# A macaron layer on one core: 24 pauses of GpSimd, ahead of the gathers of row 2 and the transfers of rows 2 and 3, are taken out

## The chip, the core and the metric

The kernel runs on one core of a Trainium2 chip. The time is the device time of one execution in microseconds (us). Nine executions of the kernel before lie between 742.82 and 747.31 us, with a median of 744.16 us.

The core has a tensor engine (PE), a vector engine (DVE), a scalar engine (ACT), GpSimd (POOL) and a sync engine (SP). Each takes its own list of instructions in order and waits on semaphores for the others. POOL issues the transfers whose rows are picked by an index (DMA_INDIRECT); SP and, at the ends, ACT issue the plain ones.

## What is computed

The input is 8 rows of 512 tokens of 128 numbers. Three sublayers follow each other, each with a layer norm ahead of it and a residual sum behind it. The first and the last are the same mixture of 8 experts; the middle one is linear attention.

```python
x = x + 0.5 * ffn(layernorm(x))      # 8 experts, the best 2 for each token, 128 -> 512 -> 128
x = x + attn(layernorm(x))           # rms norm; q, k expanded to [1, x, x*x/sqrt2]; 8 heads of 16
x = x + 0.5 * ffn(layernorm(x))      # the same weights again

def ffn(x):                          # probs = softmax(x @ gate_w.T + gate_b)
    h = relu(x @ w1[e] + b1[e])      # for the 2 best experts e of a token
    return sum(prob[e] * (h @ w2[e] + b2[e]))
def attn(x):                         # q, k, v = x @ w_q, x @ w_kv
    return ((q2 @ (k2.T @ v)) / max(q2 . sum(k2), 1e-5)) @ w_out
```

## The kernel before

**Tokens go through HBM, sorted by expert.** For each pair of rows (`Route`, from line 572 on) the kernel works out which two experts each token needs and its place in that expert's region. Then POOL writes the normed tokens into the buffer `xg` in HBM, 128 tokens to an indirect transfer (line 660): a pair of rows has 2 x 4 blocks of tokens x 2 experts, so 16 transfers. `Tiles` reads the regions back 256 tokens at a time (`rows`, line 802, issued by SP), loads the two matrices of the tile's expert (`load`, lines 816 and 818, also SP), transposes (L827), multiplies with both matrices (L843, L858), transposes back (L867) and weighs by the gate (L869). The first sublayer's results are written to the buffer `yt` by SP (L880), the last sublayer's by POOL with indirect transfers (L885).

**The middle.** When a set of rows of the first sublayer is stored, `fetch` (from line 1114 on) gathers each row's two results from `yt` with 8 indirect transfers (line 1125) into a buffer `got`, of which there are two, so the gathers of row b wait until row b-2 has been added. `added` (L1139, DVE) adds them to x; `ready` norms x for the attention; `Attention.prep` makes k, v and q; `squares` (L1018 on PE, L1022 on ACT) makes the squared features of q; `core` sums k with v in 64 small matmuls (L1035) and applies them (L1064, L1066); `quotient` (L1077 on PE, L1080 to L1082 on DVE) and `tail` (L1099 to L1107) divide, project and add to x. Rows 0 and 1 form one set of the first sublayer, rows 2 to 7 another. The last sublayer has one set of 8 rows, planned in three steps: the first step takes rows 0 to 3, the next two rows more, and the last all eight.

**The pause.** `pace()` (line 399) issues a memset of an unused tile of 128 x 192 numbers on POOL (line 402) whenever `clock.paced` is true. It is called ahead of each indirect transfer to `xg` (line 659) and ahead of each gather (line 1124). `PACED = (True, False)`: it is on while the tiles of the first sublayer run and, by line 1227, through the whole attention; it is off for rows 0 and 1 of the first sublayer and while the tiles of the last sublayer run. The memset waits for nothing but POOL itself, so the pause that belongs to a transfer runs as soon as POOL has finished the instruction before it, even where the transfer then waits for a long time.

**The order of the work** is laid down by a planner that runs while the program is built. The work is cut into streams (Python generators); `Clock.look` keeps a time for each engine from fixed costs, and the streams are advanced where their inputs are due (`deal`, `drain`, and a loop over `main` and `side` during the attention). Its costs for POOL are 1.27 us for an indirect transfer out of or into these buffers, and 0.4 us for any other instruction of POOL, the pause among them:

```python
                elif moved:
                    cost = 0.38 if e != "Pool" else 1.9 if outs[0].bass_ap.tensor.name.startswith("x_all") else 1.27
...
                else:
                    cost = 0.4
```

What the planner lays down is then fixed: at the end each instruction is tied to the one before it on its engine. So a change to POOL's list can also change where the instructions of the other engines stand.

Of the kernel before, what the change touches and what calls it, by code (L numbers as in the profile page):

```python
# [36 lines left out]
STAGES = ((4, "rows"), (3, "load"), (2, "turn"), (1, "first"), (0, "second"), (-1, "back"))  # L37
# [10 lines left out]

AHEAD = 2
EARLY = 0.5  # L50
REST = 192

SPARE = (2, 3)
# [7 lines left out]
def macaron_kernel(ctx: ExitStack, tc: tile.TileContext, x, gamma, w_q, w_kv, w_out, gate_wT, gate_b, w1, b1T, w2, b2, out):  # L61
# [49 lines left out]
    class Clock:  # L111
# [1 line left out]


        def __init__(self):
            self.lead, self.paced = LEAD, False
# [199 lines left out]
    def plan_constants():  # L316
        pb1 = psum_misc("pb1")
        nc.tensor.transpose(pb1[0 : E * NC, 0:P], b1s.rearrange("p e c -> p (e c)"), ident)
        nc.vector.memset(b1T32, 0.0)
        nc.vector.tensor_copy(b1T32[0 : E * NC, :], pb1[0 : E * NC, 0:P])  # L320
        nc.vector.tensor_copy(iota_n, iota_i)
        nc.vector.tensor_scalar(iota_2, iota_n[0:1], 2.0, None, ALU.mult)


        nc.vector.tensor_scalar(qi[:, 1:2], qi[:, 0:1], NC.bit_length() - 1, None, ALU.arith_shift_right)
        nc.vector.tensor_scalar(qi[:, 2:3], qi[:, 0:1], NC - 1, None, ALU.bitwise_and)
        nc.vector.tensor_copy(qf, qi)
# [12 lines left out]
        nc.vector.tensor_scalar(which, qf[:, 1:2], float(CAP // N), None, ALU.mult)  # L340
# [55 lines left out]

    rest_area = const.tile([P, REST], F32, name="rest_area")

    def pace():

        if clock.paced:
            nc.gpsimd.memset(rest_area, 0.0)  # L402

    def sent(i, s, g, phase):
# [167 lines left out]
    class Route:  # L572
# [5 lines left out]
        def prep(self):  # L578
# [77 lines left out]
            for t in range(C):  # L656
                for k in range(2):
                    yield "pool"
                    pace()
                    i = nc.gpsimd.indirect_dma_start(  # L660
                        xg[s][g], bass.IndirectOffsetOnAxis(rows[s][:, k, b * T + t : b * T + t + 1], 0), xn[:, t, k], None
                    )
                    sent(i, s, g, phase)

    class Tiles:


        def __init__(self, second, p, prior=None):
            self.s, self.p = int(second), p
            self.g, self.rows_in, self.whole = PHASES[self.s][p]  # L670
            self.prior = prior
            if self.whole:
                self.NF, self.NH = whole_tiles(self.rows_in) - (prior.upto if prior else 0), HALVES
            else:
# [216 lines left out]
    def tiles(ps, pool, steps, routing, sides):  # L891


        spare = SPARE[steps[0].s]
        rest = [(steps[-1], j) for j in range(steps[-1].NF - spare, steps[-1].NF)]
        seq = [(t, j) for t in steps for j in t.order if (t, j) not in rest]
        L = len(seq)
        clock.paced = PACED[steps[0].s]
        kept, keep = [], KEPT[steps[0].s]
        for t in steps:  # L900
            t.ps, t.pool = ps, pool
        for n in range(-4, L + 2):
            if n + 4 < L and (n == -4 or seq[n + 4][0] is not seq[n + 3][0]):
                at = steps.index(seq[n + 4][0])
                drain(routing[at], [s for part in routing[at + 1 :] for s in part])
            if n == -4:

                for t, j in seq[:AHEAD]:
                    t.number(j)
                    t.load(j)  # L910
            open_ones = [s for part in routing for s in part if not s.over]
            for k, (lag, stage) in enumerate(STAGES):
                if 0 <= n + lag < L:
# [6 lines left out]
                if k == len(STAGES) - 1 and (len(kept) > keep or not open_ones):  # L920
                    for u, i in kept[:2]:
                        u.store(i)
                    kept = kept[2:]
                if n >= -1:
                    deal(open_ones + sides)
        while kept:
            u, i = kept.pop(0)
            u.store(i)
        if rest:

            t = steps[-1]
            first = nc.values_load(t.regs[0:1, rest[0][1] : rest[0][1] + 1], min_val=0, max_val=NIL)
            with tc.If(first < NIL):  # L933
                blocks.append(nc.cur_bb.bb)
                for n in range(-4, len(rest) + 2):
                    for lag, stage in STAGES:
                        if 0 <= n + lag < len(rest):
                            getattr(t, stage)(rest[n + lag][1])
                            if stage == "back":
                                t.store(rest[n + lag][1])  # L940
            blocks.append(nc.cur_bb.bb)
            clock.seen = 0

    class Attention:
        def __init__(self, b):
# [168 lines left out]
    def fetch(group):  # L1114

        for u in group:
            b = u.b
            g = set_of[0][b][0]
            yield lambda: all_stored(0, g) and (b < GOT or units[b - GOT].fetched)
            u.got = work.tile([P, 2, T, D], F32, tag="got", name=f"got_{b}", bufs=GOT)  # L1120
            yield "pool"
            for t in range(T):
                for k in range(2):
                    pace()
                    i = nc.gpsimd.indirect_dma_start(  # L1125
                        u.got[:, k, t, :].bitcast(I32), None, yt[0][g].bitcast(I32), bass.IndirectOffsetOnAxis(rows[0][:, k, b * T + t : b * T + t + 1], 0)
                    )
# [167 lines left out]
```

## Time and profile before

| what | us |
|---|---|
| median of nine executions | 744.16 |
| the profiled execution's own time | 745.51 |
| its span, from the first to the last instruction | 743.7 |
| PE busy in the span | 560.7 |
| POOL busy | 306.8 |
| of that: 128 transfers to `xg` (L660) | 132.1 |
| 64 gathers (L1125) | 63.8 |
| 144 pauses (L402) | 39.5 |
| mean granted clock of PE, as a share of full speed | 0.88 |

The stages, in us from the start of the span: the first sublayer's routing and tiles until about 301; the attention from there to 514; the last sublayer's tiles from 518 to about 717; the last sums and the output until the end. Of the 144 pauses, 48 stand ahead of the transfers of rows 2 to 7 to the first sublayer, 64 ahead of the gathers, and 32 ahead of the transfers of rows 0 to 3 to the last sublayer.

How to read the lines of the trace: a row of the timeline has the start, the duration, the engine, the line of the kernel, the operation, what it writes <- what it reads, and the number of instructions merged into it; in brackets stands how long the engine had been idle before it and what ended that. "issue" means that the engine waited for nothing that the profile shows. "PEld" is the loading of weights into PE, and "SPq" is SP's list of instructions.

### The profile page before, as it was taken

The numbers are of one execution on the slowest core, as the hardware profiler recorded it, in microseconds if no ns is written. First come the engines' busy times: TensorE is split into PE (matmuls) and PEld (weight loads), VectorE is DVE, ScalarE is ACT, GpSimd is POOL, SyncE is SP. The second block draws the span as 40 slices with busy tenths as digits, with TensorE's granted clock in tenths as the row PEclk, the third lists the DMA queues.
The fourth block names the chain that finished last, engine by engine and source line by source line (L and its number), as shares of the span: only waits on it lengthen the run. The fifth ranks groups of instructions, "written<-read, shape, count | busy, mean of one in ns | idle before, by whom it ended". The sixth has DMA issues, their size and how long they took to land. (4 is left out here: it accounts for less than half of the span.)

```text
span 743.7 us, 11286 instructions
## 1 busy us (share of the span) xinstructions
PE 560.7 (75%) x3239; PEld 402.8 (54%) x3239; DVE 314.7 (42%) x1186; ACT 265.6 (36%) x587; POOL 306.8 (41%) x452
## 2 busy tenths in 40 slices
PE   3348785389879999878868879977855866999950
PEld 1237664268668888334424425432744744888840
DVE  5616352123264475125934842730532421333325
ACT  3024521024224643316545454525213412444410
POOL 3520828820820000566860390380073374445540
PEclk9999788679979999979998996996786977999995
DMA  4136525347648656111110010012423434787829
GB/s 150 51 107 162 142 85 156 102 128 208 196 125 225 193 157 165 49 36 37 39 38 0 16 40 5 12 44 70 119 84 90 141 121 134 207 226 212 223 63 335
DMA packets 89392, 87.27 MB, mean 117 GB/s; under 512 B 10152, under 2 KB 70832, under 8 KB 89328
## 3 DMA queue, kind: packets, MB, share of 16 engines
q1 hardware_dynamic: 78896, 66.16, 31.4%
q0 software_dynamic: 8320, 17.19, 7.4%
q10 hardware_dynamic: 2112, 3.18, 1.2%
q8 instruction: 27, 0.44, 0.3%
q14 instruction: 37, 0.30, 0.1%
HBM read 62.57 MB, written 23.91 MB: 116 GB/s over the span
## 5 line engine op out<-in xcount | busy, mean ns | idle before, releaser
L660 POOL DMA_INDIRECT xg<-xn_f,rows x128 | 132.1, 1032 | 187.9 <-issue 102.5
L843 PE MATMUL ph_t<-xT_t,w1t_t 128*128 128x256 f32 (+1 forms) x640 | 157.1, 393 | 1.5 <-DMA w1t_t<-in_w_dram 1.0
L858 PE MATMUL py_t<-h_t,w2t_t 128*128 128x256 f32 (+1 forms) x640 | 151.2, 381 | 2.6 <-issue 2.6
L858 PEld LDWEIGHTS py_t<-h_t,w2t_t 128*128 128x128 f32 x640 | 120.8, 201 | 19.4 <-issue 3.4
L843 PEld LDWEIGHTS ph_t<-xT_t,w1t_t 128*128 128x128 f32 x640 | 120.0, 207 | 17.9 <-DMA w1t_t<-in_w_dram 2.9
L1125 POOL DMA_INDIRECT got<-yt,rows x64 | 63.8, 997 | 149.2 <-SPq L933 95.9
L850 DVE TENSOR_SCALAR h_t<-ph_t,bias_t 128x256 f32<-128x256 f32 (+1 forms) x160 | 66.8, 459 | 127.4 <-PE ph_t L843 74.3
L860 ACT ACTIVATE yT_t<-py_t,bias_t 128x256 f32<-128x256 f32 (+1 forms) x80 | 36.6, 457 | 172.1 <-PE py_t L858 114.3
L885 POOL DMA_INDIRECT yt<-y_t,to_t x68 | 65.1, 957 | 76.9 <-DVE to_t L832 54.7
L848 ACT ACTIVATE h_t<-ph_t,bias_t 128x256 f32<-128x256 f32 (+1 forms) x160 | 64.5, 454 | 63.5 <-PE ph_t L843 42.6
L827 PE MATMUL pt_t<-ident,xt_t 128*128 128x128 f32 x148 | 32.6, 300 | 43.7 <-DVE gone_t L778 16.5
L869 DVE TENSOR_TENSOR y_t<-py_t,xt_t 128x256 f32<-128x256 f32 (+1 forms) x80 | 32.2, 403 | 64.5 <-PE py_t L867 49.8
L1035 PE MATMUL pz_a<-fac,v 128*32 128x160 f32 x512 | 36.8, 310 | 18.0 <-issue 16.8
L827 PEld LDWEIGHTS pt_t<-ident,xt_t 128*128 128x128 f32 x148 | 19.0, 150 | 49.1 <-DVE gone_t L778 16.7
L829 ACT COPY xT_t<-pt_t 128x256 f32<-128x256 f32 (+1 forms) x80 | 28.2, 353 | 43.8 <-PE pt_t L827 32.0
L558 ACT ACTIVATE xn_f<-x_all,off_f,rs_w_f 128x256 f32<-128x256 f32 x64 | 32.4, 591 | 30.8 <-DVE off_f L547 30.8
L402 POOL MEMSET rest_area<- 128x192 f32 x144 | 39.5, 274 | 0.1
L1035 PEld LDWEIGHTS pz_a<-fac,v 128*32 128x32 f32 x512 | 18.6, 109 | 36.4 <-issue 33.4
L567 PE MATMUL pt_f<-ident,xn_f 128*128 128x128 f32 x64 | 17.2, 383 | 23.5 <-ACT xn_f L558 18.0
L867 PE MATMUL py_t<-ident,yT_t 128*128 128x128 f32 x148 | 31.0, 286 | 5.0 <-ACT xT_t L829 2.5
L988 DVE TENSOR_TENSOR fac<-fac 128x896 f32<-128x896 f32 x32 | 33.1, 1082 | 0.0
L1080 DVE TENSOR_SCALAR d_a<-pd_a 128x16 f32<-128x16 f32 x16 | 2.7, 171 | 64.3 <-PE pd_a L1077 59.8
(403 smaller groups left out, 706.4 us busy)
## 6 DMA issues: line engine op xcount, KB each, us to landing
w1t_t<-in_w_dram SPq DMA_DIRECT2D x80, 256.0 KB
w2t_t<-in_w_dram SPq DMA_DIRECT2D x80, 256.0 KB
xt_t<-xg SPq DMA_DIRECT2D x68, 130.0 KB
yt<-y_t SPq DMA_DIRECT2D x36, 128.0 KB
xg<-nil SPq DMA_DIRECT2D x27, 130.0 KB
x_all<-in_x_dram SPq DMA_DIRECT2D x8, 256.0 KB
xg<-xn_f,rows POOLq DMA_INDIRECT x128
fac<-yt SPq DMA_DIRECT2D x4, 512.0 KB
```

Of the source, the lines that this page charges most:

```text
L402: nc.gpsimd.memset(rest_area, 0.0)
L660: i = nc.gpsimd.indirect_dma_start(xg[s][g], bass.IndirectOffsetOnAxis(rows[s][:, k, b * T + t : b * T + t + 1], 0), xn[:, t, k], None)
L827: nc.tensor.transpose(pt[:, bass.ts(u, P)], self.x[j][:, u, 0:D], ident)
L843: nc.tensor.matmul(ph[c // 2][:, c % 2, 0:n], lhsT=self.w[j][0][:, bass.ts(c, P)], rhs=self.xT[j], start=True, stop=True)
L848: nc.scalar.activation(h, ph[c // 2][:, c % 2, 0:n], AF.Relu, bias=bias)
L850: nc.vector.tensor_scalar(h, ph[c // 2][:, c % 2, 0:n], bias, 0.0, ALU.add, ALU.max)
L858: nc.tensor.matmul(py, lhsT=self.w[j][1][:, c, :], rhs=self.h[j][c], start=(c == 0), stop=(c == NC - 1))
L860: nc.scalar.activation(self.yT[j], py, AF.Identity, bias=self.bias[:, NC, j : j + 1])
L885: i = nc.gpsimd.indirect_dma_start(yt[self.s][self.g], bass.IndirectOffsetOnAxis(self.to[j][:, u : u + 1], 0), self.y[j][:, u, :], None)
L988: nc.vector.tensor_tensor(out, one, two, ALU.mult)
L1035: nc.tensor.matmul(sums[slot, bass.ts(k, FS)], lhsT=self.v[:, t, 2 * j + k, :], rhs=self.fac[:, t, 2 * j + k, LIN : LIN + FS], start=(t == 0),
L1125: i = nc.gpsimd.indirect_dma_start(u.got[:, k, t, :].bitcast(I32), None, yt[0][g].bitcast(I32), bass.IndirectOffsetOnAxis(rows[0][:, k, b ...
```

## The change

The pause is left out in two places: ahead of the 8 gathers of row 2 (but not of row 3), and ahead of the 16 transfers to the last sublayer of the stream that holds rows 2 and 3. That is 24 of 144 pauses. `pace` gets the row as an argument; for the first sublayer's transfers and the other gathers it is called with -1, which pauses as before.

```diff
+HURRY = 1
...
-    def pace():
-
-        if clock.paced:
+    def pace(b=-1):
+
+        if clock.paced and not (HURRY and b in (2, 3)):
             nc.gpsimd.memset(rest_area, 0.0)
...
                 for k in range(2):
                     yield "pool"
-                    pace()
+                    pace(b if s else -1)
                     i = nc.gpsimd.indirect_dma_start(
                         xg[s][g], bass.IndirectOffsetOnAxis(rows[s][:, k, b * T + t : b * T + t + 1], 0), xn[:, t, k], None
                     )
...
             for t in range(T):
                 for k in range(2):
-                    pace()
+                    pace(b if b == 2 else -1)
                     i = nc.gpsimd.indirect_dma_start(
                         u.got[:, k, t, :].bitcast(I32), None, yt[0][g].bitcast(I32), bass.IndirectOffsetOnAxis(rows[0][:, k, b * T + t : b * T + t + 1], 0)
                     )
```

The rest of the diff adds switches that are set to nothing: `LASTS = (0, 0)` is subtracted in the order of the half tiles, `MID = 0` leaves the list of tiles put aside in the first step empty, the block for the spare tiles becomes a function of its own, and a step's plan also waits (in the planner) for a flag `clock.made`, which is set once the constants have been made.

```diff
-            self.order = sorted(range(self.NT), key=lambda j: j if j < self.NF else (j - self.NF + EARLY) * self.NF / self.NH - 0.5)
+            self.order = sorted(range(self.NT), key=lambda j: j if j < self.NF else (j - self.NF + EARLY) * (self.NF - LASTS[int(second)]) / self.NH - 0.5)
...
-            yield lambda: counted[s][g] == self.rows_in and (not self.prior or self.prior.planned)
+            yield lambda: clock.made and counted[s][g] == self.rows_in and (not self.prior or self.prior.planned)
...
+        early = [(steps[0], j) for j in range(steps[0].NF - MID, steps[0].NF)] if s == 0 else []
+        seq = [(steps[0], j) for j in steps[0].order if (steps[0], j) not in early + rest]
+        cut = len(seq) if early else None
...
         plan_constants()
+        clock.made = True
```

More of the change, by code (lines that the diff above doesn't have):

```diff
@@ L50 @@
 EARLY = 0.5
+LASTS = (0, 0)
+HURRY = 1
+MID = 0
 REST = 192
@@ L115, in __init__ @@
         def __init__(self):
-            self.lead, self.paced = LEAD, False
+            self.lead, self.paced, self.made = LEAD, False, False
             self.seen, self.last, self.link = len(nc.cur_bb.bb.instructions), 0.0, {}
@@ L891, in tiles @@
     def tiles(ps, pool, steps, routing, sides):
-        spare = SPARE[steps[0].s]
-        rest = [(steps[-1], j) for j in range(steps[-1].NF - spare, steps[-1].NF)]
-        seq = [(t, j) for t in steps for j in t.order if (t, j) not in rest]
+        s = steps[0].s
+        rest = [(steps[-1], j) for j in range(steps[-1].NF - SPARE[s], steps[-1].NF)]
+        early = [(steps[0], j) for j in range(steps[0].NF - MID, steps[0].NF)] if s == 0 else []
+        seq = [(steps[0], j) for j in steps[0].order if (steps[0], j) not in early + rest]
+        cut = len(seq) if early else None
+        if early:
+            seq += [None] * 3
+        seq += [(t, j) for t in steps[1:] for j in t.order if (t, j) not in rest]
         L = len(seq)
-        clock.paced = PACED[steps[0].s]
-        kept, keep = [], KEPT[steps[0].s]
+        clock.paced = PACED[s]
+        kept, keep = [], KEPT[s]
         for t in steps:
             t.ps, t.pool = ps, pool
+        begun = None
         for n in range(-4, L + 2):
-            if n + 4 < L and (n == -4 or seq[n + 4][0] is not seq[n + 3][0]):
-                at = steps.index(seq[n + 4][0])
+            if n + 4 < L and seq[n + 4] and seq[n + 4][0] is not begun:
+                begun = seq[n + 4][0]
+                at = steps.index(begun)
                 drain(routing[at], [s for part in routing[at + 1 :] for s in part])
@@ L912, in tiles @@
             for k, (lag, stage) in enumerate(STAGES):
-                if 0 <= n + lag < L:
+                if 0 <= n + lag < L and seq[n + lag]:
                     t, j = seq[n + lag]
@@ L919, in tiles @@
                         kept.append((t, j))
-                if k == len(STAGES) - 1 and (len(kept) > keep or not open_ones):
+                if k == len(STAGES) - 1 and (len(kept) > keep or not open_ones or n == cut):
                     for u, i in kept[:2]:
@@ L925, in tiles @@
                     deal(open_ones + sides)
+            if n == cut:
+                assert not kept
+                spares(early)
         while kept:
@@ L929, in tiles, with spares @@
         if rest:
[L931 to L940, printed above, removed]
-            blocks.append(nc.cur_bb.bb)
-            clock.seen = 0
+            spares(rest)
+    def spares(rest):
+        t = rest[0][0]
+        first = nc.values_load(t.regs[0:1, rest[0][1] : rest[0][1] + 1], min_val=0, max_val=NIL)
+        with tc.If(first < NIL):
+            blocks.append(nc.cur_bb.bb)
+            for n in range(-4, len(rest) + 2):
+                for lag, stage in STAGES:
+                    if 0 <= n + lag < len(rest):
+                        getattr(t, stage)(rest[n + lag][1])
+                        if stage == "back":
+                            t.store(rest[n + lag][1])
+        blocks.append(nc.cur_bb.bb)
+        clock.seen = 0
     class Attention:
```

## The prediction

> **What bounds the kernel now.** I began with POOL's timeline, because the change touches POOL alone. It shows what a pause takes: first in the transfers of rows 2 and 3 to the last sublayer, then in the transfers of rows 4 and 5, which have none.
>
> ```profile
> 489.65 0.27 POOL L402 MEMSET rest_area<- 128x192 f32 x1
> 490.08 0.96 POOL L660 DMA_INDIRECT xg<-xn_f,rows  x1 [0.16 <-issue]
> 491.05 0.27 POOL L402 MEMSET rest_area<- 128x192 f32 x1
> 491.49 0.96 POOL L660 DMA_INDIRECT xg<-xn_f,rows  x1 [0.17 <-issue]
> ...
> 541.11 0.95 POOL L660 DMA_INDIRECT xg<-xn_f,rows  x1 [0.30 <-issue]
> 542.37 0.96 POOL L660 DMA_INDIRECT xg<-xn_f,rows  x1 [0.30 <-issue]
> ```
>
> From start to start it is 1.405 us with the pause and 1.262 without. The memset takes 0.27 us, but POOL is idle for 0.16 to 0.17 us before a transfer instead of 0.30, so a pause costs 0.143 us and not 0.27.
>
> The second view was PE's timeline beside POOL's. One step of the attention, the 64 small matmuls of L1035, shows what POOL's lists do to other engines:
>
> ```profile
> 301.63 2.39 PE L1035 MATMUL pz_a<-fac,v 128*32 128x160 f32 x64 [1.07 <-DVEq L933]
> ...
> 316.39 1.55 PE L1035 MATMUL pz_a<-fac,v 128*32 128x160 f32 x34
> 318.53 0.49 PE L1035 MATMUL pz_a<-fac,v 128*32 128x160 f32 x5 [0.58 <-issue]
> 319.99 0.50 PE L1035 MATMUL pz_a<-fac,v 128*32 128x160 f32 x5 [0.97 <-issue]
> ```
>
> With POOL silent (unit 0, at 301.6) all 64 take 2.39 us. Beside the paced gathers of rows 2 and 3, which run from 305.61 to 327.3, the same step takes from 316.39 to 327.9: PE gets 4 or 5 matmuls, then stands for up to 0.97 us, waiting for nothing that the profile shows. It recurs at 490.96 to 501 beside the transfers of rows 2 and 3. So POOL's lists hold PE back even with pauses, and until they end.
>
> The third view was the windows beside those transfers (columns: PE, PEld, DVE, ACT and POOL busy in us, each with its count; clock; DMA share; GB/s):
>
> ```profile
> 486.00:494.00 8.00, 7.36 (x80) 2.66 (x80) 2.94 (x20) 2.28 (x3) 7.17 (x12) 1.00 0.14 44
> 494.00:503.00 9.00, 5.74 (x31) 2.33 (x28) 2.16 (x13) 0.00 (x0) 7.28 (x12) 0.82 0.16 51
> ```
>
> PE starts 80 matmuls in the first 8 us, 31 in the next 9. Those 31 are little work: 64 of L1035 take 2.39 us, so about 1.2 us.
>
> The fourth view was the chain of waits where the pauses are already missing:
>
> ```profile
> 549.10 0.88 DVE h_t L850 x2
> 549.98 15.30 another core or an unknown queue
> ```
>
> The transfers of rows 4 and 5, without pauses, run from 539.85 to 562.3, and from 549.98 to 564.5 neither PE nor ACT starts anything. That speaks loudest against the change.
>
> Last, SP's waits tell what starts the last sublayer:
>
> ```profile
> SPq L816 <- PE pav_a L1066: 25.9, 1, 25.9
> ```
>
> The weights of its third tile wait until PE has ended the attention's last matmuls, at 514.49. Its first rows are asked for behind that, at 518.19, though the last transfer of rows 2 and 3 was issued by 502.3. So not the transfers but PE's attention sets the start of the last stage; from there to the end PE is the bound (81.0 of 81 us busy from 625 to 706).
>
> **The change, part by part.** The 8 gathers of row 2: POOL ran the first of their pauses at 209.40, ahead of 95.93 us of idle time, so it costs nothing. Seven lie between gathers. The period there is 1.385 us (305.61, 307.00, 308.38); no gather without a pause is in the trace, so I take the gather's 0.95 and the transfers' 0.30 gap, 1.25 us. That is 7 x 0.134 = 0.9 us. Bounds: 0 (row 3's paced gathers follow, and PE's hindrance at 316 to 328 might simply keep its length) and 7 x 0.27 = 1.9 us (the whole memset). I take 0.9: the nearest row, the transfers, gives half of the memset. It lies on the path: row 3's gathers end 0.9 us sooner, and with them the hindrance that holds PE in unit 1's L1035 until 327.9. DVE's sum for row 2 (330.34) stands behind the quotient of unit 0, which waits 15.7 us for PE behind that same step. What is late next is that sum, and behind it the gathers of row 4, which start at 332.02.
>
> The 16 transfers: the first pause ran at 446.34, 29 us before its transfer. Fifteen lie between: 15 x 0.143 = 2.1 us. They end at 500.2 instead of 502.3. Nobody waits for their data (covered by 12 us until 514.49; without that cover it would be the same 2.1 us). But PE is freed from its crawl 2.1 us sooner, with units 6 and 7 still to be finished and the end of them on the path. Bounds: a gain of 15 x 0.27 = 4.1 us, and a loss of 8.1 us, worked out below as the slow rival. I take the gain of 2.1, because the stretch from 494 on is already nearly a standstill, and ending it sooner is what is left to change.
>
> One of these 16 transfers (480.11) takes 5.02 us beside DVE's four multiplications of L988, 4.1 us in all. [...] By the rows alone each list of 16 met one such group of L988, with one transfer held, and the sum stays as it is.
>
> The rest of the diff does nothing: with `LASTS` and `MID` at zero the orders are the same lists, and DVE's constants (L333, at 26.5 us) stand ahead of the first plan's first instruction (L699, at 29.0) already.
>
> The sum: 0.9 + 2.1 = 3.0 us. The profiled execution took 745.51 us, 1.8 around its span of 743.7; it becomes 742.5, with a span of 740.7. It lay 1.35 above the median of nine, so against the median: 744.16 - 3.0 = 741.1 us. With the bounds of a gain (1.9 + 4.1) it is 738.2.
>
> **The rivals.** *The planner lays the work down differently, for the better.* It charges 0.4 us for a pause, so it now sees row 2's gathers 8 x 0.4 = 3.2 us sooner, and may put row 2's sum ahead of the quotient of unit 0. Then it need not wait for PE until 329.5, and POOL loses its pause ahead of row 4:
>
> ```profile
> 332.02 0.95 POOL L1125 DMA_INDIRECT got<-yt,rows  x1 [4.41 <-DVE x_all L1139]
> ```
>
> For it: the sum's data landed about 12 us before it ran. Against it: other engines' lists are full there. Price: 3.0 + 4.4 = 7.4 us, 736.8.
>
> *The order turns out worse.* The same shift moves the steps of L1035 against POOL's lists. Only unit 0's runs free (2.39 us); unit 2's, from 364.14 to 367.1, and unit 6's, from 477.4 to 481.3, get by lightly. One of these falling into a list, as unit 7's does (490.96 to 500.7, 9.7 us), costs about 9.7 - 2.4 = 7.3 us: 744.16 - 3.0 + 7.3 = 748.5. Against it: five of eight already lie there, so there is more to win than to lose.
>
> *Nothing moves.* PE's attention is bound by its own and DVE's work, POOL's earlier end is absorbed, and the first rows of the last stage are asked for at 518 as before: 744.2. For it: the 12 us of cover. Against it: PE stands idle exactly while POOL issues.
>
> *Slower: the full standstill moves into the attention.* Among the transfers without pauses the stop begins 549.98 - 539.85 = 10.1 us after the first and lasts until 2.3 us after the last (562.26 to 564.53). Put on rows 2 and 3 it would reach from 486.0 to 502.5. The work PE did there before, 7.36 us up to 494 and 1.2 after, would follow at 502.5, so what was reached at 503 is reached at 511.1: 8.1 us later. With the 0.9 of the gathers it is 744.16 + 8.1 - 0.9 = 751.4. It decides from the point at which the stop begins: before 494 it costs, from there on the crawl covers it. For it: both lists without pauses beside tiles show such a stop. Against it: those stood beside SP's loads (75 to 127 GB/s, against 28 here), and the held transfer at 480 to 485 gives the others 5 us to catch up; counted from its end, the stop would begin at 485.6 + 10.1 = 495.7, under the crawl.
>
> **How the numbers follow.** The forecast (741.1) 0.33; a better order (736.8) 0.20; nothing (744.2) 0.14; the standstill (751.4) 0.20; a worse order (748.5) 0.13. The likeliest case by itself reaches from 738.2, where each pause is worth its whole memset, to 742.7, where half of the gain is absorbed. The gains hold 0.53 and the losses 0.33; since the losses go further, the range must reach past 748.5 to the standstill's 751.4, and below to the better order's 736.8, a little past each since both are sums: 735.5 to 751.5. A measurement of this kernel can tell about 0.2%, 1.5 us, from no change. Faster by more than that (under 742.7): 0.53. Within it: 0.14. Slower: 0.33.
>
> **What would show it.** Right: 120 memsets of L402; gathers of row 2 at 1.25 us from start to start, transfers of rows 2 and 3 at 1.26; unit 1's L1035 ending near 327 and unit 7's crawl ending about 2 us sooner; SP's wait at L816 ending near 511.5; everything behind it shifted by the same amount. Wrong: a stop of PE of 10 us or more between 476 and 503 (the standstill); a different order of DVE's list around L1139 and L1080 (the planner); or L816 still let go at 514.5 (nothing moves). [...]

## The result, and the profile after

The kernel after takes 753.6 us (median of 20 executions, 747.76 to 757.0) beside 744.16 us for the kernel before (62 executions). The ratio is 1.0134, with a 95% interval of 1.0114 to 1.0153: **9.4 us slower**, and above the range of the prediction. The profiled execution took 750.93 us, with a span of 749.0 us; it has 120 pauses. The lines of the code have moved: L1035 is now L1052, L1064 and L1066 are L1081 and L1083, L660 is L664, L1125 is L1142, L988 is L1005, L816 is L820; in some of the experiments the lines lie 1 to 3 further on. Unit n is the attention of row n.

POOL did what the diff says. Its timeline in the kernel after: row 2's gathers, the first of row 3, and the first transfers of rows 2 and 3.

```profile
304.30 0.95 POOL L1142 DMA_INDIRECT got<-yt,rows  x1 [95.58 <-SPq L950]
305.56 0.94 POOL L1142 DMA_INDIRECT got<-yt,rows  x1 [0.30 <-issue]
...
313.98 0.28 POOL L406 MEMSET rest_area<- 128x192 f32 x1
314.42 0.95 POOL L1142 DMA_INDIRECT got<-yt,rows  x1 [0.17 <-issue]
...
478.43 0.96 POOL L664 DMA_INDIRECT xg<-xn_f,rows  x1 [42.07 <-issue]
479.70 0.95 POOL L664 DMA_INDIRECT xg<-xn_f,rows  x1 [0.31 <-issue]
```

From start to start a gather without a pause takes 1.25 us and a transfer 1.26, as predicted. But the other engines fared differently. Here is PE's timeline for the step of unit 1 beside the gathers (64 matmuls; in the kernel before it lasted from 316.39 to 327.9):

```profile
318.55 1.01 PE L1052 MATMUL pz_a<-fac,v 128*32 128x160 f32 x21
320.61 0.33 PE L1052 MATMUL pz_a<-fac,v 128*32 128x160 f32 x2 [1.05 <-issue]
322.00 0.30 PE L1052 MATMUL pz_a<-fac,v 128*32 128x160 f32 x1 [1.06 <-issue]
...
338.12 1.83 PE L1052 MATMUL pz_a<-fac,v 128*32 128x160 f32 x20 [0.27 <-issue]
```

PE now gets one or two matmuls every 0.7 to 1.4 us, where it got 4 or 5, until POOL's list ends. That list is longer: rows 2, 3 and 4 follow each other without a gap, 24 gathers from 304.30 to 336.1. The windows beside the transfers of rows 2 and 3 (columns as in the prediction's windows of the kernel before):

```profile
486.00:494.00 8.00, 0.11 (x2) 0.00 (x0) 0.00 (x0) 0.00 (x0) 6.17 (x7) 0.50 0.17 58
494.00:503.00 9.00, 1.66 (x7) 1.33 (x8) 0.41 (x3) 0.87 (x2) 3.40 (x4) 0.50 0.09 30
```

PE was busy for 7.36 and 5.74 us of these 8 and 9 us before, and for 0.11 and 1.66 now. The chain of waits says the same of this list, and of the next one, where the kernel before had a stop of 15.30 us too:

```profile
480.14 20.96 another core or an unknown queue
...
555.85 3.09 issue
559.91 15.67 issue
```

A full standstill has come, up to 501.1. SP's wait shows how late the attention ends:

```profile
SPq L820 <- PE pav_a L1083: 13.7, 1, 13.7
```

Its end, PE's last matmuls of L1083, is at 516.3, 1.8 us later than before, while the whole span is 5.3 us longer. So a part of the loss arises behind the attention, where the diff takes out no pause.

The runs below stood on five chips. On two of them the kernel before takes 607 us, and no stop beside a list of POOL's is seen (beside the 16 transfers of rows 2 and 3 PE's longest idle time is 0.85 us in e1); on the others it takes 744 to 759 us ("a chip with stops": PE stands for 15.23 us in the first result and for 14.99 in e13). Each run is compared only with the kernel before on its own chip. In the tables the times are medians of all executions, but the ratios leave out those in a slow state, over 1.5% above the quickest of the same kernel, so that a ratio can differ from the quotient of the times by up to 0.4%.

### The profile page after: what moved, and what is told of

It is laid out like the page before. It is cut to its first block, busy times and chain, and to the rows that moved or that the text cites. A ratio compares the mean times of both kernels' runs of the same rounds, so it can differ in the third digit from the quotient of the medians.

```text
span 749.0 us, 11262 instructions
## 1 busy us (share of the span) xinstructions
PE 546.6 (73%) x3239; PEld 399.4 (53%) x3239; DVE 314.0 (42%) x1186; ACT 264.6 (35%) x587; POOL 295.0 (39%) x428
## 4 chain that ended last, share of the span: by engine, by line
PE 36%; issue 6%; ACT 5%; another core or an unknown queue 5%; DMA 3%; DVE 2%; POOL 1%; SPq 1%; DVEq 0%; ACTq 0%; POOLq 0%
PE ph_t L847 8%; PE py_t L862 6%; PE pz_a L1052 4%; PE pav_a L1081 3%; PE pf_a_rest L1035 2%; PE pav_a L1083 2%; DMA fac<-yt 2%; PE po_a L1122 1%; DMA yt<-y_t,to_t 1%; PE pkv_a L982 1%; PE pt_t L831 1%; PE pd_a L1094 1%; PE pl_f L597 1%; PE py_t L871 1%
## 5 line engine op out<-in xcount | busy, mean ns | idle before, releaser
L664 POOL DMA_INDIRECT xg<-xn_f,rows x128 | 126.4, 988 | 149.3 <-issue 83.0
L847 PE MATMUL ph_t<-xT_t,w1t_t 128*128 128x256 f32 (+1 forms) x640 | 158.1, 394 | 2.9 <-DMA w1t_t<-in_w_dram 2.6
L862 PE MATMUL py_t<-h_t,w2t_t 128*128 128x256 f32 (+1 forms) x640 | 149.5, 378 | 1.7 <-issue 1.7
L847 PEld LDWEIGHTS ph_t<-xT_t,w1t_t 128*128 128x128 f32 x640 | 120.8, 209 | 19.4 <-DMA w1t_t<-in_w_dram 4.2
L862 PEld LDWEIGHTS py_t<-h_t,w2t_t 128*128 128x128 f32 x640 | 119.3, 199 | 17.8 <-issue 2.5
L1142 POOL DMA_INDIRECT got<-yt,rows x64 | 64.2, 1003 | 158.3 <-SPq L950 95.6
L833 ACT COPY xT_t<-pt_t 128x256 f32<-128x256 f32 (+1 forms) x80 | 28.2, 354 | 52.2 <-PE pt_t L831 21.3
L1052 PE MATMUL pz_a<-fac,v 128*32 128x160 f32 x512 | 35.5, 348 | 15.3 <-issue 14.1
L1052 PEld LDWEIGHTS pz_a<-fac,v 128*32 128x32 f32 x512 | 21.2, 124 | 30.3 <-issue 28.6
L406 POOL MEMSET rest_area<- 128x192 f32 x120 | 32.9, 275 | 0.1
L1005 DVE TENSOR_TENSOR fac<-fac 128x896 f32<-128x896 f32 x32 | 32.9, 1084 | 0.0
L871 PEld LDWEIGHTS py_t<-ident,yT_t 128*128 128x128 f32 x148 | 20.5, 147 | 14.4 <-ACT xT_t L833 7.0
```

The costliest lines, as they stand in the source:

```text
L664: i = nc.gpsimd.indirect_dma_start(xg[s][g], bass.IndirectOffsetOnAxis(rows[s][:, k, b * T + t : b * T + t + 1], 0), xn[:, t, k], None)
L847: nc.tensor.matmul(ph[c // 2][:, c % 2, 0:n], lhsT=self.w[j][0][:, bass.ts(c, P)], rhs=self.xT[j], start=True, stop=True)
L862: nc.tensor.matmul(py, lhsT=self.w[j][1][:, c, :], rhs=self.h[j][c], start=(c == 0), stop=(c == NC - 1))
L871: nc.tensor.transpose(pb[:, bass.ts(u, P)], self.yT[j][:, bass.ts(u, P)], ident)
L1052: nc.tensor.matmul(sums[slot, bass.ts(k, FS)], lhsT=self.v[:, t, 2 * j + k, :], rhs=self.fac[:, t, 2 * j + k, LIN : LIN + FS], start=(t == 0),
L1142: i = nc.gpsimd.indirect_dma_start(u.got[:, k, t, :].bitcast(I32), None, yt[0][g].bitcast(I32), bass.IndirectOffsetOnAxis(rows[0][:, k, b ...
```

## The experiments

**What the diff does to the order.** With `HURRY` at 0 the program is that of the kernel before, instruction for instruction, so the rest of the diff is inert. With only the transfers' pauses gone, the order of every other instruction is the one of before as well. With only row 2's gathers' pauses gone it is already that of the kernel after, so the 8 gathers alone make the new order. There are thus two orders and two lots of pauses, and they can be crossed. "Stop" and "order" are the two theories at first.

### Crossing pauses and order

e1: the transfers' pauses alone. e2: the gathers' pauses alone. e3: the new order with all pauses. e4: the gathers' pauses alone, in the old order.

```diff
 e1
-                    pace(b if b == 2 else -1)
+                    pace(-1)
 e2
-        if clock.paced and not (HURRY and b in (2, 3)):
+        if b == 5 or clock.paced and not (HURRY and b in (2, 3)):
...
-                    pace(b if s else -1)
+                    pace(5 if s and b in (2, 3) else -1)
 e3
-                if e not in self.free:
+                if e not in self.free or i.name in self.unseen:
...
+        if clock.paced or b in (2, 3):
+            i = nc.gpsimd.memset(rest_area, 0.0)
+            if HURRY and b in (2, 3):
+                clock.unseen.add(i.ins.name)
 e4
+        elif clock.paced:
+            clock.look()
+            clock.free["Pool"] += 0.4
...
-                    pace(b if s else -1)
+                    pace(-1)
```

> Only the 16 pauses ahead of the transfers of rows 2 and 3 go; row 2's gathers keep theirs, and the order of all instructions is that of the kernel before. Two theories. 'Stop': 16 transfers without pauses bring PE, DVE and ACT to a full stop that lasts until 2 to 3 us after the last of them, and that is the whole loss. It expects a stop from about 484 to 503 in PE, and 750 to 753 us (my price for it of 8.1 us, on 744.2). 'Order': the loss comes from the new order that the planner lays down, and the transfers' pauses matter little. It expects no stop of more than 3 us there and 742 to 744.5 us.

> Only the 8 pauses of row 2's gathers go; the 16 transfers keep theirs. The planner lays all other instructions down as in the kernel after. 'Stop' expects no full stop beside the transfers. At 478 us the kernel after had ended 228 of the attention's 256 matmuls pav_a, the kernel before 196, so with the stop gone this is the quickest so far: 744.2 less some 4 to 10 us, 734 to 740. 'Order' expects the time of the kernel after, 752 to 755.

> All 144 pauses stand, but the planner doesn't count the 24, so every other instruction stands where it stands in the kernel after. This is the new order alone. 'Stop' expects 735 to 741 us, some 1 us above the run with row 2's pauses gone. 'Order' expects 752 to 755.

> The order of the kernel before (the planner still counts 0.4 us where a pause would stand), with the 8 pauses of row 2's gathers left out. Both theories expect little. My prediction's first term: 0.9 us less, 743.3; a third idea, that the 16 gathers from 304 on come to a full stop as well when half of them have no pauses, would cost PE the matmuls L1035 of unit 1 that it ran from 316 to 326, some 2 to 5 us: 746 to 749.

| run, beside before at 607.03 us | us | ratio, 95% interval |
|---|---|---|
| e1 transfers' pauses gone (old order) | 608.59 | 1.0017, 0.9995 to 1.0040 |
| e2 gathers' pauses gone (new order) | 618.72 | 1.0201, 1.0170 to 1.0233 |
| e3 new order, all pauses | 618.26 | 1.0177, 1.0147 to 1.0206 |
| e4 gathers' pauses gone, old order | 606.96 | 0.9993, 0.9964 to 1.0022 |

These stood on a chip of the 607 us kind. In e1 nothing stops: the window over its 16 transfers has PE at work nearly throughout.

```profile
389.00:414.00 25.00, 23.64 (x286) 11.16 (x285) 14.18 (x52) 15.10 (x29) 19.65 (x16) 1.00 0.13 42
```

So "stop" couldn't be tried there; "order" is borne out in its sign (its times were stated for the other kind of chip): the new order alone, with every pause in place, costs 11 us. Where it loses is shown by the same window of e2 and then of e4, in the last stage:

```profile
470.00:500.00 30.00, 22.82 (x109) 17.97 (x107) 11.49 (x58) 7.52 (x18) 22.68 (x25) 0.83 0.66 194
```

```profile
470.00:500.00 30.00, 27.91 (x145) 23.03 (x144) 13.88 (x65) 9.99 (x24) 22.35 (x24) 1.00 0.75 219
```

and by SP's wait for the indirect transfers ahead of the tiles' rows, of e2 and then of e4 (total, times, longest):

```profile
SPq L806 <- DMA xg<-xn_f,rows: 27.5, 9, 16.2
```

```profile
SPq L809 <- DMA xg<-xn_f,rows: 15.5, 11, 3.7
```

The first transfer of rows 4 and 5 starts at 451.99 in e2 and at 437.82 in e4, though the attention ends at the same time (its last matmuls start at 410.7 and 411.4). The gate of these rows (L597, `pl_f`) stands behind the first tile's first matrix (L847) on PE's list in the new order; in the old one it stands ahead of that matrix, right behind the tile's first two transposes. In the kernels before and after it is the same. PE's timeline of before, then of after:

```profile
521.64 0.66 PE L827 MATMUL pt_t<-ident,xt_t 128*128 128x128 f32 x2 [5.28 <-DMA xt_t<-xg]
522.10 3.42 PE L593 MATMUL pl_f<-gwT,xnT_f 128*128 128x8 f32 x16
...
528.69 2.76 PE L843 MATMUL ph_t<-xT_t,w1t_t 128*128 128x256 f32 x8
```

```profile
523.17 1.08 PE L831 MATMUL pt_t<-ident,xt_t 128*128 128x128 f32 x4 [6.33 <-DMA xt_t<-xg]
...
527.07 3.14 PE L847 MATMUL ph_t<-xT_t,w1t_t 128*128 128x256 f32 x8
...
533.58 1.95 PE L597 MATMUL pl_f<-gwT,xnT_f 128*128 128x8 f32 x16
```

Their first transfers of rows 4 and 5 start at 539.85 (before) and 552.49 (after).

### The kernel after again, and the old order without pauses

e5 is the kernel after. e6 has its 24 pauses gone in the old order, e7 all 144; both charge the 0.4 us as e4 does. e8 has all pauses, and the planner counts 0.143 us for each.

```diff
 e7
-        if clock.paced and not (HURRY and b in (2, 3)):
+        if clock.paced and False:
 e8
-                    cost = 0.4
+                    cost = 0.143 if i.name in self.rests else 0.4
```

> The kernel after, unchanged, beside the kernel before. The first four runs stood on a chip on which the kernel before takes 607 us instead of 744, and there the two kernels with the new order lost 1.8 to 2.0% while the transfers' pauses alone cost 0.2%. 'Order' expects, on a chip like that, 1.018 to 1.024 (618 to 621 us), and on one like that of the first result 1.013 again. 'Stop' expects that the part that the stop adds is missing on the 607 us chip: under 1.005.

> All 24 pauses go as in the kernel after, but the planner still counts 0.4 us for each, so all other instructions stand as in the kernel before. 'Order' expects the time of the kernel before on either chip: 0.997 to 1.004. 'Stop' expects the stop's 8 us where the chip shows stops (1.010 to 1.013 of 744 us), and 1.000 to 1.004 where it doesn't.

> The order of the kernel before, and none of the 144 pauses is made. If pauses protect the other engines on this chip, the 120 further ones must cost much: 16 transfers cost 1.6 us, so 48 more ahead of the first sublayer's transfers and 56 ahead of gathers at that price make 10 us or more. If pauses do nothing here but take POOL 0.143 us each, then the time falls or stays: the lists of 32 transfers and 40 gathers end 4.6 and 5.7 us sooner, of which little is waited for: 0.990 to 1.000.

> All 144 pauses stand, and the planner counts 0.143 us for each, which is what one was seen to cost, instead of 0.4. That makes a third order. 'Order' says that the time moves by some per cent for the order alone and that its sign can't be told from POOL's own time: outside 0.995 to 1.005, in either direction. If instead the order that the kernel after has is slow for a reason of its own (row 2's sum early), a mere change of the charge should stay within 0.995 to 1.005.

| run, beside before at 758.63 us | us | ratio, 95% interval |
|---|---|---|
| e5 kernel after | 768.74 | 1.0142, 1.0087 to 1.0198 |
| e6 all 24 gone, old order | 753.06 | 0.9941, 0.9906 to 0.9977 |
| e7 all 144 gone, old order | 774.56 | 1.0198, 1.0129 to 1.0268 |
| e8 a third order, all pauses | 757.16 | 1.0002, 0.9960 to 1.0045 |

This chip shows stops. e6 is the kernel that my sum was made for, and it is quicker: the old order carries the change, the new one doesn't. e5 and e6 lack the same 24 pauses and differ in the order alone, and 768.74 - 753.06 = 15.7 us lie between them. "Stop" had expected a loss for e6 and is off; "order" had expected 0.997 to 1.004, which the interval just reaches. And e8 falls against "any new order moves the time": a third order is worth nothing either way. Its profile has both signs, though: the gate of rows 4 and 5 stands behind the first tile there too (544.16 and 534.84) and all that follows the attention is long, while the attention itself is short (206.6 and 238.8 us, measured as in the last table below). e7 shows that pauses do protect on this chip: without any, the time is 774.56 us beside 758.63, and there are stops beside the gathers too, as in e7's chain of waits:

```profile
358.27 6.47 another core or an unknown queue
```

Why no standstill in e6? Windows over the transfers, of e6 and then of the kernel after:

```profile
486.00:511.00 25.00, 20.03 (x185) 8.49 (x184) 9.70 (x28) 7.93 (x15) 19.70 (x16) 0.91 0.13 41
```

```profile
478.00:501.00 23.00, 5.74 (x76) 2.48 (x72) 0.91 (x6) 0.58 (x1) 15.31 (x16) 0.66 0.14 47
```

The same 16 transfers at the same pace, and PE does 20.03 us of work beside the one and 5.74 beside the other. Two things differ. In e6 the fourth transfer is held beside DVE's four multiplications of `fac`, as it was before; in the kernel after the last of these ran at 466.55 to 470.6, ahead of the list, and no transfer takes over 0.96 us. And the instruction behind PE's step `pe_t`: first POOL's and PE's timeline of e6, then PE's of the kernel after.

```profile
490.51 5.30 POOL L667 DMA_INDIRECT xg<-xn_f,rows  x1 [0.30 <-issue]
```

```profile
497.49 0.19 PE L764 MATMUL pe_t<-take_t,ev_t 33*1 33x9 f32 x2
497.61 0.62 PE L1084 MATMUL pav_a<-sq_a_(0, 0)_5018,zT_a 128*32 128x512 f32 x2
```

```profile
485.91 0.20 PE L761 MATMUL pe_t<-take_t,ev_t 33*1 33x9 f32 x2
501.34 1.12 PE L1116 MATMUL po_t_a<-ident,on_a 128*128 128x128 f32 x4 [15.23 <-DVE regf_t L764]
```

In e6 PE has matmuls of the attention next, which wait for nothing. In the kernel after the next one is let go, by the profile, by DVE's `regf_t`, and DVE starts nothing before 501.13. DVE stands in e6 too (11.41 us, up to 510.36), but PE's next matmuls don't need it. Which of the two differences decides wasn't tried by itself.

### Rows 4 and 5 early, or late

If the place of that gate is what costs, moving it alone should win the time back. e9 keeps the planning loop of the attention going until the gate of rows 4 and 5 is laid down, which brings the attention's last tails ahead of the first tile as well; the transfers' pauses stay gone. e11 does the opposite to the kernel before. e10 repeats e2 and e12 repeats e1.

```diff
 e9
+            if s and b == 4:
+                clock.made = 2
...
-        while not core.over:
+        while not core.over or clock.made != 2:
 e11
-HURRY = 1
+HURRY = 0
...
-            yield lambda: all(u.done for u in units[b : b + n])
+            yield lambda: all(u.done for u in units[b : b + n + (b == 4)])
```

> The kernel after, with one change: the attention's planning loop goes on until the gate's matmuls for rows 4 and 5 of the last sublayer have been laid down, so these stand ahead of the first tile on PE's list, not behind it. 'Late routing' (the new order loses because the transfers of rows 4 and 5 to the last sublayer come 12 to 17 us later, and its second step starves): they should come back by 8 us or more, and the time should fall by 5 to 11 us below that of the kernel after, to a ratio of 0.997 to 1.007. 'Spread' (the new order is worse in many small places): 1.012 to 1.020 stays. 'Stop' (on a chip that shows stops): the stop at 480 to 501 stays and so does the loss, 1.010 to 1.014.

> The new order with row 2's pauses gone and the 16 transfers' pauses kept, as in the second run. On a chip that shows no stops: 1.020 again. On one that does, where the kernel after is at 1.013 to 1.014: 'Stop' expects that the standstill ahead of the last sublayer goes with the pauses back, and the ratio falls below 1.005. 'Late routing' expects that the ratio stays at 1.010 or more, since the transfers of rows 4 and 5 come as late as before.

> The kernel before with all 144 pauses, and the planner lets the routing of rows 4 and 5 to the last sublayer begin only when unit 6 is finished too, not with units 4 and 5. That puts its gate's matmuls behind the first tiles, later still than in the kernel after. Attention up to its last matmuls is laid down as before. 'Late routing' expects 1.015 to 1.035, more than in the kernel after as the transfers come later still. 'Spread' and 'Stop' expect little, under 1.008.

> The order of the kernel before, the 16 transfers without pauses, as in the first run. On a chip without stops 1.000 to 1.004 again. On one with stops, where both lots of pauses gone in this order gave 0.994: my prediction's second term expects 2.1 of those 4.5 us from here, 0.996 to 0.998; if it's the gathers that gave all of it, 0.999 to 1.003; 'Stop' expects 1.008 or more.

| run, beside before at 756.90 us | us | ratio, 95% interval |
|---|---|---|
| e9 after, gate of rows 4 and 5 early | 758.51 | 1.0037, 1.0002 to 1.0072 |
| e10 new order, transfers paced | 766.24 | 1.0167, 1.0114 to 1.0221 |
| e11 old order, gate late | 757.92 | 1.0053, 1.0009 to 1.0097 |
| e12 old order, transfers not paced | 758.75 | 1.0053, 1.0009 to 1.0098 |

The kernel after itself was not run on this chip. Beside its 1.2 to 1.4% on the others, e9 has won most of the loss back. e10 shows that the new order stays slow with the transfers' pauses back, as "late routing" had it and "stop" not. But e11 misses: its transfers of rows 4 and 5 start 27 us later than in e12 (the first at 575.99 and 548.79), and it loses 0.5%, not 1.5 to 3.5%. So lateness alone isn't the price. Nor is PE's wait for the first rows alone: in e11 it is 6.41 us, with the last tails and the gate behind it as in the kernel after, and yet e11 takes 232.4 us from the attention's last matmuls to the end, beside 237.8 in e10 and 231.5 in e12.

e12 falls between the stated ranges: not the gain that my second term had, and a smaller loss than "stop" expected. Its loss of 0.1 to 1.0% is barely clear of nothing (over all executions the medians differ by 0.2%). No standstill is in it: over the same window as e6, PE is busy for nearly as long.

```profile
486.00:511.00 25.00, 19.76 (x184) 8.19 (x182) 10.24 (x30) 7.59 (x15) 19.66 (x16) 0.88 0.13 41
```

### Both edits on one chip

e13 is the kernel after, e14 has the transfers' pauses back, e15 the gate early, and e16 both.

> The kernel after, beside the next three on one chip. 1.013 to 1.014 where the chip shows stops (measured twice); where it doesn't, 1.018 to 1.022, as the two other kernels with this order had there.

> The kernel after with the 16 transfers' pauses back. 'Stop' expects it 0.5 to 1% quicker than the kernel after on a chip with stops. 'Late routing' expects no gain against it, within 0.4% either way, since the paced transfers hold PE back nearly as much and the last stage starts its routing as late.

> The kernel after with the gate of rows 4 and 5 laid down ahead of the first tile. 'Late routing' expects it 7 to 11 us quicker than the kernel after on the same chip, of either kind: 1.002 to 1.006 with stops, 1.003 to 1.010 without. If that gain came only from the chip on which it was measured, it lies within 4 us of the kernel after.

> Both edits: the gate of rows 4 and 5 early, and the 16 transfers' pauses back (only row 2's gathers without). 'Stop' expects 5 to 8 us less than the run without these pauses on a chip with stops, which would be 0.993 to 0.997 and the quickest kernel. 'Late routing' expects the same time as that run, within 3 us.

| run, beside before at 743.59 us | us | ratio, 95% interval |
|---|---|---|
| e13 kernel after | 753.11 | 1.0117, 1.0068 to 1.0165 |
| e14 and transfers paced | 748.09 | 1.0089, 1.0049 to 1.0129 |
| e15 and gate early | 745.13 | 1.0028, 0.9993 to 1.0063 |
| e16 and both | 741.40 | 0.9961, 0.9924 to 0.9997 |

The early gate is worth 753.11 - 745.13 = 8.0 us, or 748.09 - 741.40 = 6.7 with pauses; the intervals overlap in neither pair, and "late routing" had expected 7 to 11. The transfers' pauses are worth 5.0 or 3.7 us; here the intervals overlap in both pairs, but taken directly from the executions of the two kernels the means differ by 4.5 and 3.9 us, each with a standard error of 1.3. That is what "stop" expected of e14; of e16 it expected 5 to 8 us, and "late routing" at most 3, so both miss there. Together 11.7 us, and **e16 is quicker than the kernel after**, and than the kernel before by 0.4% (0.03 to 0.76%, barely clear of nothing). What the early gate does is seen in PE's timeline of e13 and then of e15:

```profile
520.76 0.66 PE L1116 MATMUL po_t_a<-ident,on_a 128*128 128x128 f32 x4
527.74 1.09 PE L831 MATMUL pt_t<-ident,xt_t 128*128 128x128 f32 x4 [6.32 <-DMA xt_t<-xg]
...
537.72 1.95 PE L597 MATMUL pl_f<-gwT,xnT_f 128*128 128x8 f32 x16
```

```profile
517.58 0.66 PE L1118 MATMUL po_t_a<-ident,on_a 128*128 128x128 f32 x4
...
523.98 1.95 PE L597 MATMUL pl_f<-gwT,xnT_f 128*128 128x8 f32 x16
...
527.85 0.63 PE L833 MATMUL pt_t<-ident,xt_t 128*128 128x128 f32 x2
```

In e13 PE stands 6.32 us for the first rows of the last stage, with the last tails of the attention and the gate behind them. In e15 this work fills the wait, and the first transfer of rows 4 and 5 goes out at 541.02, not 556.66. What the pauses do is in the windows of e13 and then e14 over the 16 transfers:

```profile
484.00:506.00 22.00, 5.17 (x72) 2.36 (x68) 0.91 (x6) 0.58 (x1) 15.03 (x16) 0.69 0.15 49
```

```profile
482.00:506.00 24.00, 13.11 (x126) 7.47 (x122) 3.28 (x18) 2.02 (x4) 19.10 (x31) 0.67 0.13 44
```

### The two terms in the old order

e17 repeats e4, and e18 repeats e6.

> The order of the kernel before, only the 8 pauses of row 2's gathers gone. My prediction's first term: 0.9 us less, 0.998 to 1.000. If the gathers made the whole gain of the kernel that has none of the 24 pauses, on a chip with stops: 0.990 to 0.996. On one without stops 0.999 again.

> The order of the kernel before, all 24 pauses gone. My prediction's sum: 3.0 us less, 0.996, as the first such run gave (0.994). If the transfers' pauses cost 0.5% when they go, as the other run has it, this lies 0.3 to 0.6% above the run beside it; if 'Stop' and the gathers cancel, 0.998 to 1.002. On a chip without stops 0.998 to 1.003.

They came to a chip of the 607 us kind (before 607.35): e17 606.52 us, 0.9992 (0.9969 to 1.0014), and e18 607.54 us, 1.0011 (0.9988 to 1.0034). There the 24 pauses are worth nothing that can be measured. The gathers alone, in the old order, were not run on a chip with stops.

### The stages in the profiles

Each profile gives two lengths: from row 2's first gather to the start of the attention's last matmuls (L1066 and its later lines), called the attention here, and from there to the end, called the last stage. Means, in us, on the chips with stops (without e7, e8 and e11, whose pauses or orders are others):

| stage | kernels | mean (lowest to highest) |
|---|---|---|
| attention | old order: before, e6, e12 | 209.2 (207.8 to 210.9) |
| attention | new order, transfers not paced: after, e5, e9, e13, e15 | 215.6 (210.9 to 219.4) |
| attention | new order, transfers paced: e10, e14, e16 | 209.9 (208.4 to 212.4) |
| last stage | old order: before, e6, e12 | 231.4 (230.3 to 232.4) |
| last stage | new order: after, e5, e10, e13, e14 | 234.9 (231.9 to 238.0) |
| last stage | new order, gate early: e9, e15, e16 | 227.6 (227.1 to 228.1) |

From the old order to that of the kernel after, the attention gets longer by 215.6 - 209.2 = 6.4 us, of which 215.6 - 209.9 = 5.7 go when the transfers have their pauses back; these I put down to the standstill. The last stage gets longer by 234.9 - 231.4 = 3.5. Together 9.9 us, beside the 9.4 of the result. These are single profiles from several chips, and the ranges are some us wide, so it is partly luck that the sum comes out this close. On one chip alone, the attention takes 214.5 and 214.2 us in e13 and e15, and 208.4 and 209.0 in e14 and e16, with the pauses back. On the 607 us chip of the first four runs the attention is equally long in e1, e2 and e4 (161.7 each; 163.6 in e3), and the last stage takes 204.3 and 204.6 us in e2 and e3 against 195.1 and 196.1 in e1 and e4: the loss lies there.

## Why the prediction was wrong, point by point

- **The pause's cost** (0.143 us a transfer, 0.134 a gather) was right, to 0.01 us.
- **The step that failed first is the frame of the sum: it was made in the order of before.** I knew that the planner would see row 2's gathers 3.2 us sooner, but I left a new order to the rivals. The new order comes from the planner's charge alone (e3). In the order that the sum was made for, the change gained 0.6% or 4.5 us on a chip with stops (e6; 0.2 to 0.9%), where I forecast 3.0, and nothing on a 607 us chip (e18). The same 24 pauses gone, the new order takes 15.7 us more (e5 against e6).
- **Term A (0.9 us):** row 2's gathers did end sooner. But PE's hindrance in unit 1 didn't end with them; it lasts to 339.88 now and not to 327.9, since row 4's gathers follow without a gap. Where the term was tried in the old order, on the 607 us chips, it is within noise (e4, e17).
- **Term B (2.1 us)** failed: "the stretch from 494 on is already nearly a standstill, ending it sooner is what is left to change". In the new order PE's standstill began 7.7 us after the first transfer (478.43 to 486.1), and the pauses' return was worth 3.7 to 5.0 us. In the old order the kernel without these pauses alone lost 0.5% (0.1 to 1.0) on one chip (e12), where this term forecast a gain; e6, without the gathers' pauses as well, gained on another. The 31 matmuls from which I priced the loss are not all of L1035; 26 are.
- **The standstill rival** named the event and its window (486.0 to 502.5 forecast; 486.1 to 501.3 measured for PE). That the start fits so well is luck: the list began 2.5 us later than before, and the stop 2.4 us sooner after it. Its size was put too high (8.1 us against 5.7, 5.0 or 3.7). I set against it that the held transfer gives the others 5 us to catch up. In the old order, with the held transfer, there was indeed no standstill (e6, e12); in the new order no transfer was held, and it came. That the held transfer is the reason isn't shown.
- **The held transfer.** In each list of 16 I counted on one transfer held beside DVE's four multiplications, as in the kernel before (5.02 us); in e6 it took 5.30. In the kernel after none of the 16 was held, each took 0.96 us at most: the multiplications had ended at 470.6, 7.8 us ahead of the list. With one transfer held PE did 20.03 us of work in 25 (e6), with none 5.74 in 23. What holds such a transfer, no run here shows.
- **A better order** came in its mechanism and not in its gain. DVE's sum for row 2 did move ahead, to 316.48, and POOL's 4.41 us of idle time are gone. But PE only got a longer list of gathers to crawl beside, and the quotient of unit 0 (L1080, now L1097) came at 341.04 instead of 329.50.
- **A worse order** had the right sign and the wrong place. I had priced a step of L1035 that falls into a list of POOL's, at 7.3 us. Unit 1's did get 9.8 us longer (from 11.5 to 21.3), but the attention as a whole did not where the transfers keep their pauses (209.9 us against 209.2). The new order's own cost lies in the last stage: 3.5 us by the table, about 9 on the 607 us chip. Bringing the last tails and the gate of rows 4 and 5 ahead of the first tile wins 6.7 to 8.0 us (e13 to e16); e11 shows that their place alone isn't the whole reason.
- **The range** took the rivals one at a time. The worse order and the standstill came together (the standstill was seen in the new order only), and their sum lies above 751.5.

**Still open:** why some chips show stops and others don't, with the same program; why the standstill comes in the new order and not in the old (the held transfer, or what stands next on PE's list); whether the early gate gains by filling PE's wait or by the earlier transfers (e11 speaks against either alone); which lot of pauses gave e6 its 0.6%, since e12 with one of them lost 0.5% on another chip, and the other lot alone was not run on a chip with stops.

## What to carry to other kernels

Where a planner lays down the order from costs, first work out whether an edit changes the order, and hold the order fixed to measure the edit: here the kernel without the same 24 pauses was 0.6% quicker than before in one order and 1.4% slower in the other, on the same chip. An argument that something covers a stall ("the held transfer lets the others catch up") belongs to an order; if the order can move, the cover can. And rivals that can happen together must be added in the range.

## What the runs showed of the hardware

- On the chips where the kernel before takes 744 to 759 us, PE, DVE and ACT are seen to start less beside lists of POOL's indirect transfers. In the kernel after PE gets one or two matmuls every 0.7 to 1.4 us beside the gathers (320.61 to 337.43); beside the unpaced transfers it stands for 15.23 us (486.1 to 501.3), and up to 501.1 DVE has stood for 20.99 us and ACT for 21.44. On the two chips where it takes 607 us lists run at the same pace (1.26 us from start to start in e4) and no such stop is seen: in e17 and e18 PE's longest idle time in the attention and the last stage is the wait for that stage's first rows, 5.56 and 4.92 us. The same program, without the transfers' pauses in the old order, has PE at work for 23.64 of 25 us beside the list there (e1) and for 19.76 of 25 on a chip with stops (e12). The new order without these pauses was not run on a 607 us chip.
- In the new order, with a pause of 0.27 us in each 1.4 us, a crawl was seen in place of such a stop: 13.11 us of PE's work in 24 us (e14), beside 5.17 in 22 without these pauses (e13). In the old order there was no such stop beside these transfers without pauses either (PE at work for 20.03 and 19.76 of 25 us in e6 and e12).
- In the kernel after PE and ACT start nothing from 486.1 to 501.0, and no transfer is held. PE waits for DVE there by the profile, but ACT's next instruction reads what PE had written by 486.1 and starts at 501.09:

  ```profile
  501.09 0.42 ACT L1060 COPY z_a<-pz_a 128x320 f32<-128x320 f32 x1 [21.44 <-remote]
  ```

  What the mechanism is, no run here shows.
